# Adding into the residual by transfer: an attention projection, a branch and mixed streams in a two-layer kernel

## The chip, the cores and the metric

The kernel runs on one core of one Trainium2 chip. The metric is device time in microseconds (us) of one execution, and lower is better. The time before is the median of three runs.

## The reference

Two layers are applied to a residual `x` of shape 2 x 1024 x 512 (batch, token, channel), everything in 32-bit floats. In both layers an attention and a second part read the same layer-normalized `xn`, and both are added to `x`:

```python
xn = layernorm(x)
x = x + L0_attn(xn) + L0_ffn(xn)      # layer 0
xn = layernorm(x)
x = x + L1_attn(xn) + L1_ffn(xn)      # layer 1

def L0_attn(x):                       # one head of 128, no mask
    q, k, v = split(x @ Wqkv + bqkv)
    return softmax(q @ k.T / sqrt(128)) @ v @ Wo + bo

def L0_ffn(x):                        # 4 streams of 128 channels
    xr = x * rsqrt(mean(x * x) + eps)
    H_res  = sinkhorn(xr @ W_res.T + base, 50 iterations)   # 4 x 4 a token
    H_pre  = softmax(xr @ W_pre.T + ...)                    # 4 a token
    H_post = softmax(xr @ W_post.T + ...)                   # 4 a token
    H_res  = (1 - g) * I + g * H_res
    y      = sum_n H_pre[n] * x_stream[n] @ W_branch        # the branch
    return sum_j H_res[i, j] * x_stream[j] + H_post[i] * y  # streams i
```

Layer 1 is a causal attention with 32 query heads in 8 groups, whose keys and values come from a low-rank projection, over the 1024 tokens of each batch. Its second part is a linear layer with eight low-rank experts, of which each token takes two. These parts are not changed.

## The kernel before, in words

**Layout.** The residual lies in SBUF for the whole run as sixteen tiles `acc[b, t]` (batch b of 2, token tile t of 8), 128 tokens x 512 channels in 32-bit floats each, 256 KB. They are loaded with `x` and everything is added to them in place; the last addition to a tile is followed by its store. Matmuls are done on pairs of 16-bit floats (a high and a low part, three products for one), so that most results are written twice: once as the high part by ScalarE (ACT) and once as the low part by VectorE (DVE) or GpSimd (POOL).

**Order.** The program names the order; a scheduler that simulates the engines then fixes each engine's own order within the dependencies, so that an edit at one place can move instructions of every engine. Tiles come from pools with a fixed number of buffers by tag; a new tile of a tag waits until the oldest buffer's readers are done. The tag that matters here is `f2k` (128 x 512 in 32-bit floats, FB = 4 buffers). It serves, among others:

- the weights fetched by POOL's queue (`fetch`, L717) and split into high and low parts by POOL (`split_pool`, L97 to L99, behind a low part of a softmax row on DVE, L338)
- the attention output of layer 0 on its way to its two parts (`ao` in `attn0_out`, written at L502, read at L504 and L505)
- the normalized tile of batch 1 in layer 0 (`normed_T`, L242, then L247 on ACT and L249 on POOL or DVE, then a transposing transfer into `big`)
- the branch's products (`branch0_add`, L477) and the mixed streams (`stream_at`, L661).

**Layer 0, batch 0 and 1.** `front0` normalizes and projects to queries, keys, values and the logits of the 4 x 4 matrices. `attn0_rows` computes softmax rows: scores on PE (L91), exponentials on ACT (L300), the low parts on POOL (L336) or DVE (L338), transposes by transfer (into `PT`). `attn0_out`, once for each half of a batch, multiplies by the values (PE L373), and then for each of four token tiles multiplies with `Wo` (L510, L512) and adds the result from PSUM to the residual on DVE (L514). `branch0` computes `y` for each tile (ACT L463, POOL L464); `branch0_add` spreads it over the four streams on POOL (L477) and adds it on POOL (L481). For batch 0 the branch adds stand right behind the attention; for batch 1 they are spread over the first steps of layer 1, each behind a low part on DVE (`behind(..., True)` is a wait on that instruction).

The Sinkhorn iteration of batch 0 (`chain_dve`, L604 to L611; its kernels are recalculated once at L596) runs on DVE in small instructions between the other work of layer 0, and ends in `Hm[0]` (L555). That of batch 1 (`chain_pool`) runs on POOL and DVE in the first half of layer 1's first group.

**Mixing.** `mix0_units` loads a tile of `x` again, normalizes it, and adds the four streams, each weighted with its column of `Hm`. In one form ACT makes the four weighted copies of a stream (L661) and POOL adds them to the residual (L662); in the other, DVE does both in one instruction a copy (L670; ACT prepares a PSUM tile at L642). Batch 0 mixes at the end of layer 0: tiles 1, 3, 6 and 7 in the first form, the others in the second. Batch 1 mixes all eight tiles in the first form while layer 1 of batch 0 runs, and there every L662 waits behind a low part on DVE:

```python
add = G.tensor_tensor(acc[b, t], acc[b, t], m, ALU.add)      # L662
if b:
    behind(add, last_low[0], True)
```

**Layer 1** normalizes batch 0 (L242 again, then `big<-wo` transposes), and runs sixteen groups (two batches of eight) of 32 softmax steps; each step's place also carries the next group's weight fetches and splits, query projections, value products (`av`, L373), output blocks, and the extra work of the other batch. The padding of short softmax rows is written by POOL (`Phl`, L342) before the row is transposed (L343, issued by SyncE, SP).

Of the kernel before, what the change touches and what calls it, by code (L numbers as in the profile page):

```python
# [11 lines left out]
AF = mybir.ActivationFunctionType  # L12
ALU = mybir.AluOpType
# [3 lines left out]
P = 128  # L17
# [3 lines left out]
H = 512  # L21
# [7 lines left out]
FB, PB, LB, XB, WB = 4, 3, 3, 4, 9  # L29
# [25 lines left out]
def tile_model(ctx: ExitStack, tc: tile.TileContext, out: bass.AP, a: dict):  # L55
# [3 lines left out]
    V, A, G = nc.vector, nc.scalar, nc.gpsimd  # L59
# [7 lines left out]
    def T(tag, shape, dt=F32, bufs=None):  # L67
        count[0] += 1
        kw = {} if bufs is None else {"bufs": bufs}
        return sb.tile(shape, dt, tag=tag, name=f"{tag}_{count[0]}", **kw)  # L70
# [4 lines left out]
    def PP(shape=(P, 512)):  # L75
        count[0] += 1
        return ps.tile(list(shape), F32, tag="pp", name=f"pp_{count[0]}", bufs=BP)

    def bc(ap, axis, n):
        return ap.unsqueeze(axis).to_broadcast(  # L80
            [*ap.shape[:axis], n, *ap.shape[axis:]])
# [43 lines left out]
    acc = {}  # L125
# [60 lines left out]
    last_hi, last_lo, last_low = [None], [None], [None]  # L186

    def after(*insts):

        st = ExitStack()  # L190
        for i in insts:
            st.enter_context(tc.issue_after(i.ins))
        return st

    def behind(i, j, wait=False):

        kind = mybir.DependencyClass.Sync if wait else mybir.DependencyClass.NoSync
        tc.add_manual_dep(i.ins, j.ins.name, mybir.DependencyInfo(
            kind, mybir.DependencyReason.DATA), reason="behind")

    def rsqrt(y, ve, tag):

        t = T(tag, list(ve.shape), bufs=2)
        A.activation(t, ve, AF.Ln)
        A.activation(y, t, AF.Exp, scale=-0.5)
        V.tensor_tensor(t, y, y, ALU.mult)
        V.tensor_tensor(t, t, ve, ALU.mult)
        V.tensor_scalar(t, t, -0.5, 1.5, ALU.mult, ALU.add)
        V.tensor_tensor(y, y, t, ALU.mult)
# [51 lines left out]
    def srow():  # L261
        count[0] += 1
        return ps.tile([P, 512], F32, tag="s", name=f"s_{count[0]}", bufs=BS)
# [68 lines left out]
    def rows_lo(Pm, r, W, pool, hl, dst):  # L332
        whole, hi, los, pad = hl
        for a0, a1, lo in los:
            if pool:
                G.tensor_tensor(lo, Pm[:, a0:a1], hi[:, a0:a1], ALU.subtract)  # L336
            else:
                last_low[0] = V.scalar_tensor_tensor(lo, Pm[:, a0:a1], r[:, 1:2], hi[:, a0:a1],  # L338
                                                     ALU.mult, ALU.subtract)
        if pad is not None:  # L340

            behind(G.memset(pad, 0.0), last_low[0])  # L342
        nc.sync.dma_start_transpose(dst[:, :whole.shape[1] // P], whole)  # L343
# [17 lines left out]
    def out_tile():  # L361
        count[0] += 1
        return ps.tile([P, 512], F32, tag="av", name=f"av_{count[0]}", bufs=BV)

    def attn_out(p, Vh, PT, nj, mixed=None):


        full = nj - (mixed is not None)
        todo = [(Vh(j, l), PT(r * nj + j)) for j in range(full) for l, r in PASSES]
        if mixed is not None:  # L370
            todo += [(mixed(l), PT(full)) for l in range(2)]
        for k, (v, pt) in enumerate(todo):
            nc.tensor.matmul(p, v, pt, start=(k == 0), stop=(k == len(todo) - 1))  # L373
# [99 lines left out]
    def branch0_add(b, t, y4, hh):  # L473

        y = y4
        y4 = T("f2k", [P, 4, P], bufs=FB)
        mul = G.tensor_tensor(y4, bc(y, 1, 4), bc(hh[:, t, 1, :], 2, P), ALU.mult)  # L477
        if b:
            behind(mul, last_low[0], True)
        af = acc[b, t]  # L480
        G.tensor_tensor(af, af, y4.rearrange("p i c -> p (i c)"), ALU.add)  # L481

    def attn0_rows(b, half, Q, K, between=lambda: None):
        PTs = []
# [9 lines left out]
    def attn0_out(b, half, Vh, PTs):  # L494

        p = out_tile()
        for k in range(2):
            attn_out(p[:, 256 * k:256 * k + 256], lambda j, l: Vh[:, j, l, :],
                     lambda n: PTs[k][:, n].rearrange("p a b -> p (a b)"), NT)
        ao = T("f2k", [P, 512], bufs=FB)  # L500
        bv = bqkv[:, 2:3]
        A.activation(ao, p, AF.Identity, bias=bv, scale=1.0 / PSCALE)  # L502
        hl = T("wo", [P, 2, 512], F16, bufs=WB)
        A.activation(hl[:, 0], ao, AF.Copy)  # L504
        G.tensor_tensor(hl[:, 1], ao, hl[:, 0], ALU.subtract)  # L505
        for q in range(4):
            t = 4 * half + q
            p = PP()
            for r in range(2):
                nc.tensor.matmul(p, row, bo[:, r], start=(r == 0), stop=False)  # L510
            for k, (l, r) in enumerate(PASSES):
                nc.tensor.matmul(p, hl[:, l, q * P:(q + 1) * P], wo0[:, r, :],  # L512
                                 start=False, stop=(k == 2))
            V.scalar_tensor_tensor(acc[b, t], p, 1.0 / 1024.0, acc[b, t], ALU.mult, ALU.add)  # L514

    def sinkhorn(b, lg):

# [106 lines left out]
    def mix0_units(b, t, rs, pool):  # L624


        got = {}

        def load():
            if b == 0 and t >= 4:  # L630
                if t % 2 == 0:
                    xr_more[t] = T("P", [P, 2, H], bufs=PB)
                xr = got["xr"] = xr_more[t & ~1][:, t % 2]
            else:
                xr = got["xr"] = T("xr", [P, H], bufs=XB)
            with after(t0):
                nc.sync.dma_start(xr, a["x"][(b * NT + t) * P:(b * NT + t + 1) * P, :])
            if b == 0:
                A.activation(xr, xr, AF.Identity, scale=rs[:, 2, t:t + 1], bias=rs[:, 1, t:t + 1])
                if not pool:  # L640
                    got["d"] = srow() if t < 4 else PP()
                    A.activation(got["d"], acc[b, t], AF.Copy)  # L642
                return
            with tc.issue_after(p0.ins):
                behind(G.tensor_scalar(xr, xr, rs[:, 2, t:t + 1], rs[:, 1, t:t + 1], ALU.mult, ALU.add),
                       last_low[0], True)

        def stream(j):
            if b == 0 and (not pool or j > 1):
                with after(*(last_rs[:1] if pool else last_rs[1:] if j else last_mix)):  # L650
                    stream_at(j)
            else:
                stream_at(j)

        def stream_at(j):
            xj = got["xr"][:, j * P:(j + 1) * P]
            by = [Hm[b][:, t, i, j:j + 1] for i in range(NC)]
            if pool:
                m = T("f2k", [P, H], bufs=FB)
                for i in range(NC):  # L660
                    A.activation(m[:, i * P:(i + 1) * P], xj, AF.Copy, scale=by[i])  # L661
                add = G.tensor_tensor(acc[b, t], acc[b, t], m, ALU.add)  # L662
                if b:
                    behind(add, last_low[0], True)
                return

            for i in range(NC):
                sl = slice(i * P, (i + 1) * P)
                dst = acc[b, t] if j == NC - 1 else got["d"]
                last_stt[0] = V.scalar_tensor_tensor(dst[:, sl], xj, by[i], got["d"][:, sl], ALU.mult, ALU.add)  # L670

        return [load] + [lambda j=j: stream(j) for j in range(NC)]
# [384 lines left out]
    PTs = attn0_rows(0, 0, *f0[0][:2], lambda: adv(CA))  # L1057
    ys0 = branch0(0, *f0[0][3:5], lambda: adv(CB))
    attn0_out(0, 0, f0[0][2], PTs)
    PTs = attn0_rows(0, 1, *f0[0][:2], lambda: adv(CA))  # L1060
    attn0_out(0, 1, f0[0][2], PTs)
    for t in range(NT):
        branch0_add(0, t, ys0[t], f0[0][4])
# [3 lines left out]
    for half in range(2):  # L1067
        if half:
            kv0[1][0]()
            kv0[1][1]()  # L1070
        for hh in (2 * half, 2 * half + 1):
            load_q(0, hh)
        PTs = attn0_rows(1, half, *f0[1][:2], lambda: adv(CD))
        attn0_out(1, half, f0[1][2], PTs)
# [60 lines left out]
    for t in range(NT):  # L1135
        put(1, 2 * t, lambda t=t: branch0_add(1, t, y4s[t], f0[1][4]))
# [93 lines left out]
```

## Time and profile before

| | |
|---|---|
| median of three runs | 1851.93 us (1847.24, 1851.93, 1852.3) |
| the profiled execution, its time | 1847.82 us |
| its span | 1846.1 us, so 1.7 us lie around it |
| mean granted clock of PE | 0.976 |
| busy, PE | 1708.1 us (93%), 11394 matmuls |
| busy, DVE | 1473.8 us (80%) |
| busy, ACT | 1189.0 us (64%) |
| busy, POOL | 871.5 us (47%) |
| POOL L662 | 48 of median 1.272 us, 196.5 to 837.4 us |
| POOL L481 | 16 of median 1.277 us, 93.4 to 324.8 us |
| DVE L514 | 16 of median 0.681 us, 91.9 to 193.9 us |
| first PE matmul of layer 1 | at 223.38 us |

The profile is of one execution. Its page gives busy times, the span in 40 slices of 46 us with the busy tenths of each engine, DMA queues, the chain of work that ended last, and the costliest groups of instructions. The trace behind it answers for one stretch, line or wait. In a row of the timeline the first number is the start in us and the second the duration, "x3" counts instructions that follow each other, and the brackets give the idle time just before on that engine and the instruction that ended it. In a row of the waits the engine and instruction that waited stand first, then the releaser, then the total in us, the number of waits and the longest. POOL's issuing of DMAs (some 0.6 us each) is not counted as busy.

### The profile page before, as it was taken

The numbers are of one execution on the slowest core, as the hardware profiler recorded it, in microseconds if no ns is written. First come the engines' busy times: TensorE is split into PE (matmuls) and PEld (weight loads), VectorE is DVE, ScalarE is ACT, GpSimd is POOL, SyncE is SP. The second block draws the span as 40 slices with busy tenths as digits, with TensorE's granted clock in tenths as the row PEclk, the third lists the DMA queues.
The fourth block names the chain that finished last, engine by engine and source line by source line (L and its number), as shares of the span: only waits on it lengthen the run. The fifth ranks groups of instructions, "written<-read, shape, count | busy, mean of one in ns | idle before, by whom it ended". The sixth has DMA issues, their size and how long they took to land. (4 is left out here: it accounts for less than half of the span.)

```text
span 1846.1 us, 35011 instructions
## 1 busy us (share of the span) xinstructions
PE 1708.1 (93%) x11394; PEld 1038.2 (56%) x11394; DVE 1473.8 (80%) x4170; ACT 1189.0 (64%) x2917; POOL 871.5 (47%) x1460
## 2 busy tenths in 40 slices
PE   4666399999999999999999999999999999999998
PEld 2434146566666655566555566665666665665565
DVE  7988868888888877887577798898787877778675
ACT  3848656767665767886366667657566767666564
POOL 5568628878766464647254233324142323235200
PEclk9888699999999999999999999999999999999999
DMA  7435225756565656456484656557565665666455
GB/s 212 84 54 130 61 64 113 162 109 142 112 145 102 147 116 143 100 133 147 82 166 99 131 110 141 111 128 162 142 141 125 142 123 129 130 143 126 103 118 118
DMA packets 685034, 228.15 MB, mean 124 GB/s; under 512 B 665633, under 2 KB 665761, under 8 KB 684850
## 3 DMA queue, kind: packets, MB, share of 16 engines
q1 hardware_dynamic: 669394, 178.65, 47.2%
q0 software_dynamic: 13152, 43.07, 8.3%
q10 hardware_dynamic: 2304, 4.20, 0.7%
q8 instruction: 89, 1.46, 0.3%
q14 instruction: 95, 0.78, 0.2%
HBM read 52.81 MB, written 4.19 MB: 31 GB/s over the span
## 5 line engine op out<-in xcount | busy, mean ns | idle before, releaser
L300 ACT ACTIVATE P<-P,nm 128x1024 f32<-128x1024 f32 (+31 forms) x528 | 391.4, 742 | 278.1 <-DVE nm L292 253.4
L338 DVE SCALAR_TENSOR_TENSOR Phl<-P,r,Phl 128x64 f16<-128x64 f32 (+16 forms) x627 | 462.9, 763 | 79.0 <-ACT Phl L330 73.3
L91 PE MATMUL s<-K,Q 128*128 128x512 f16 (+22 forms) x2400 | 440.5, 317 | 19.8 <-DVE nm L292 10.5
L373 PE MATMUL av<-PT,V 128*128 128x256 f16 x3456 | 422.6, 273 | 12.2 <-DMA PT<-Phl 6.8
L373 PEld LDWEIGHTS <-V 128*128 128x128 f16 x3456 | 336.8, 98 | 95.1 <-DMA PT<-Phl 9.7
L330 ACT ACTIVATE Phl<-P,r 128x1024 f16<-128x1024 f32 (+31 forms) x515 | 368.8, 731 | 17.1 <-DMA PT<-Phl 2.0
L91 PE MATMUL pp<-wo,ao 128*128 128x512 f16 x1536 | 370.2, 380 | 3.3 <-ACT ao L107 3.2
L91 PE MATMUL pp<-big,wq 128*128 128x512 f16 x1536 | 368.6, 380 | 0.0
L97 POOL TENSOR_SCALAR f2k<-f2k 128x512 f32<-128x512 f32 x164 | 110.5, 675 | 512.3 <-DVE Phl L338 461.4
L91 PEld LDWEIGHTS <-Q 128*128 128x128 f16 x2400 | 223.9, 98 | 177.3 <-issue 29.6
L91 PEld LDWEIGHTS <-wq 128*128 128x128 f16 x1536 | 149.1, 98 | 166.8 <-issue 2.7
L91 PEld LDWEIGHTS <-ao 128*128 128x128 f16 x1536 | 149.7, 98 | 158.4 <-ACT ao L107 5.0
L91 PEld LDWEIGHTS <-big 128*128 128x128 f16 x1824 | 120.9, 99 | 87.8 <-DMA big<-wo 40.6
L292 DVE CUSTOM_DVE_ANT_0 P<-s,mask,nm 128x272 f32<-128x272 f32 (+15 forms) x256 | 157.7, 617 | 11.1 <-PE s L91 3.1
L296 DVE TENSOR_SCALAR_CACHE_REDUCE P<-s 128x512 f32<-128x512 f32 (+15 forms) x272 | 152.3, 562 | 11.9 <-PE s L91 10.4
L324 DVE RECIPROCAL r<-r 128x1 f32<-128x1 f32 x528 | 79.3, 155 | 78.6 <-ACT P L300 75.4
L325 ACT ACTIVATE r<-r 128x1 f32<-128x1 f32 x528 | 94.9, 192 | 68.3 <-DVE r L324 67.6
L107 ACT ACTIVATE ao<-av 128x512 f16<-128x512 f32 x128 | 75.0, 586 | 83.9 <-PE av L373 80.6
L342 POOL MEMSET Phl<- 128x192 f16 (+1 forms) x320 | 55.7, 189 | 153.0 <-DMA PT<-Phl 86.8
L292 DVE CUSTOM_DVE_ANT_0 P<-s,mask 128x32 f32<-128x32 f32 (+15 forms) x256 | 105.1, 430 | 19.0 <-PE s L91 18.6
L91 PE MATMUL pp<-big,big 128*128 128x128 f16 (+2 forms) x816 | 103.9, 283 | 17.5 <-DVE sk L606 12.7
L777 DVE SCALAR_TENSOR_TENSOR acc<-pp,acc 128x512 f32<-128x512 f32 x128 | 87.1, 681 | 31.6 <-PE pp L91 31.1
(266 smaller groups left out, 2064.3 us busy)
## 6 DMA issues: line engine op xcount, KB each, us to landing
f2k<-in_Wq POOLq DMA_DIRECT2D x64, 256.0 KB, 3.1
f2k<-in_WoT POOLq DMA_DIRECT2D x64, 256.0 KB, 3.3
PT<-Phl SPq DMA_TRANSPOSE x528, 3.2
acc<-in_x SPq DMA_DIRECT2D x16, 256.0 KB, 5.3
f2k<-in_Wup POOLq DMA_DIRECT2D x16, 256.0 KB, 3.4
xr<-V SPq DMA_DIRECT2D x32, 128.0 KB, 2.3
out<-acc ACTq DMA_DIRECT2D x16, 256.0 KB, 2.7
xr<-in_x SPq DMA_DIRECT2D x12, 256.0 KB, 5.1
```

The lines of the kernel that those rows point to most:

```text
L91: nc.tensor.matmul(dst, lhs(l), rhs(r), start=(i == 0 and j == 0), stop=(i == n - 1 and j == 2))
L97: first = G.tensor_scalar(stage, stage, scale, 1.0, ALU.mult, ALU.mult)
L107: A.activation(hl_hi, src, AF.Copy, scale=scale)
L292: last_row[0] = V.tensor_tensor_reduce(Pm[:, o:o + w], pt[:, :w], mask[:, 512 - w:], -scale, first, ALU.add, ALU.min, nm[:, k:k + 1])
L296: last_row[0] = V.tensor_scalar(Pm[:, o:o + w], pt[:, :w], -scale, first, ALU.mult, ALU.min, accum_out=nm[:, k:k + 1])
L300: A.activation(Pm[:, :W], Pm[:, :W], AF.Exp, bias=last, scale=-1.0, accum_out=r[:, 0:1])
L324: V.reciprocal(r[:, 1:2], r[:, 0:1])
L325: A.activation(r[:, 1:2], r[:, 1:2], AF.Copy, scale=PSCALE)
L330: A.activation(hl[1], Pm[:, :W], AF.Copy, scale=r[:, 1:2])
L338: last_low[0] = V.scalar_tensor_tensor(lo, Pm[:, a0:a1], r[:, 1:2], hi[:, a0:a1], ALU.mult, ALU.subtract)
L373: nc.tensor.matmul(p, v, pt, start=(k == 0), stop=(k == len(todo) - 1))
L777: V.scalar_tensor_tensor(acc[b, t], p, 1.0 / 256.0, acc[b, t], ALU.mult, ALU.add)
```

## The change

A helper issues a transfer on POOL's queue that adds its source to its destination. It is used at three places: for the projection of layer 0's attention (all sixteen tiles; ACT first copies the PSUM result, scaled, to an `f2k` tile), for the branch (all sixteen tiles) and for the mixed streams of batch 1 (32 transfers, four to each tile, without the wait behind DVE's low part). Batch 0's streams stay with POOL's addition. So 64 transfers of 256 KB from SBUF to SBUF are added, and 16 DVE instructions and 48 POOL additions go; 16 ACT copies come in. Two transfers to one tile follow each other by a wait on the first one's landing, and a source buffer is free when its transfer has landed.

```diff
+    def add_to(dst, src):
+
+        return G.dma_start(dst, src, accum_op=ALU.add)
+
...
     def branch0_add(b, t, y4, hh):
...
-        af = acc[b, t]
-        G.tensor_tensor(af, af, y4.rearrange("p i c -> p (i c)"), ALU.add)
+        add_to(acc[b, t], y4.rearrange("p i c -> p (i c)"))
...
     def attn0_out(b, half, Vh, PTs):
...
-            V.scalar_tensor_tensor(acc[b, t], p, 1.0 / 1024.0, acc[b, t], ALU.mult, ALU.add)
+            y = T("f2k", [P, H], bufs=FB)
+            A.activation(y, p, AF.Copy, scale=1.0 / 1024.0)
+            add_to(acc[b, t], y)
...
         def stream_at(j):
...
                 for i in range(NC):
                     A.activation(m[:, i * P:(i + 1) * P], xj, AF.Copy, scale=by[i])
-                add = G.tensor_tensor(acc[b, t], acc[b, t], m, ALU.add)
                 if b:
-                    behind(add, last_low[0], True)
+                    add_to(acc[b, t], m)
+                else:
+                    G.tensor_tensor(acc[b, t], acc[b, t], m, ALU.add)
                 return
```

## The prediction

> **What bounds the kernel now.** I read the 40 slices first, then the busy times by stretch, then the timeline of the stretch where PE isn't full, then the waits and the DMA rows.
>
> ```profile
> PE   4666399999999999999999999999999999999998
> DVE  7988868888888877887577798898787877778675
> ```
>
> The first five slices (some 230 us) are layer 0: PE is half idle and DVE, with the Sinkhorn chain of batch 0 between its other work, is the fullest engine. From slice six on PE is full. So a delay in layer 0 is paid in full, unless it disappears before PE's first matmul of layer 1, and a gain on DVE, ACT or POOL later is worth at most the little that PE idles there. The stretches give the sizes (columns: busy us of PE, PEld, DVE, ACT, POOL with counts, clock, DMA share, GB/s):
>
> ```profile
> 92.00:138.00 46.00, 28.34 (x197) 17.16 (x196) 40.04 (x137) 19.02 (x37) 28.85 (x27) 0.81 0.31 56
> 138.00:184.00 46.00, 32.04 (x236) 18.99 (x233) 40.53 (x134) 37.44 (x78) 37.12 (x43) 0.85 0.52 127
> 184.00:235.00 51.00, 20.63 (x97) 9.27 (x96) 46.07 (x141) 31.69 (x91) 32.72 (x34) 0.70 0.23 59
> 235.00:600.00 365.00, 355.80 (x2331) 215.59 (x2330) 294.56 (x831) 234.29 (x588) 254.39 (x532) 0.99 0.57 120
> 600.00:880.00 280.00, 269.22 (x1873) 167.07 (x1871) 221.84 (x583) 211.43 (x566) 158.25 (x232) 1.00 0.59 131
> ```
>
> The streams of batch 1 are mixed in 600 to 880: there PE idles 280 - 269.22 = 10.8 us. That is all that this part can win. In layer 0 the seam between the batches decides (timeline, POOL, then ACT, then PE; start, duration, instruction, idle before and releaser):
>
> ```profile
> 102.39 4.04 POOL L477 TENSOR_TENSOR f2k<-ao,hh 128x512 f32<-128x512 f32 x4
> 106.38 4.94 POOL L481 TENSOR_TENSOR acc<-acc,f2k 128x512 f32<-128x512 f32 x4
> 111.27 1.06 POOL L477 TENSOR_TENSOR f2k<-ao,hh 128x512 f32<-128x512 f32 x1
> 112.26 1.17 POOL L249 TENSOR_TENSOR wo<-f2k,wo 128x512 f16<-128x512 f32 x1
> ```
> ```profile
> 108.91 0.81 ACT L242 ACTIVATE f2k<-acc,rsa 128x512 f32<-128x512 f32 x1 [10.14 <-POOL acc L481]
> ```
> ```profile
> 116.68 1.58 PE L91 MATMUL pp<-big,big 128*128 128x152 f16 x11 [12.73 <-DVE sk L606]
> ```
>
> ACT's first normalized tile of batch 1 (L242) waits 10.14 us, because it wants one of the four f2k buffers and a branch add of batch 0 still reads it. After it come ACT L247, POOL L249, a transpose and PE's first matmul of batch 1, 7.8 us later. So f2k buffers, not arithmetic, set the start of batch 1, and the change makes every accumulated tile hold such a buffer until a DMA has landed.
>
> **Price of a landing.** No accumulating DMA and no SBUF-to-SBUF copy of 256 KB is in this trace. The nearest rows (KB each, median us from issue to landing):
>
> ```profile
> q0 software_dynamic: 13152, 43.07, 8.3%
> ...
> f2k<-in_Wq POOLq DMA_DIRECT2D x64, 256.0 KB, 3.1
> ...
> acc<-in_x SPq DMA_DIRECT2D x16, 256.0 KB, 5.3
> xr<-V SPq DMA_DIRECT2D x32, 128.0 KB, 2.3
> ```
>
> Low end 2.3 (a copy inside SBUF, half the bytes), high end 5.3 (sixteen loads in a burst). I take 4.0: POOL's own fetch of 256 KB at 3.1, and one more source read. Queue q0 used 8.3% of 1846.1 us for 43.07 MB, 164 pieces of 256 KB, so 153.2 / 164 = 0.93 us a piece, and 3.1 + 0.93 = 4.0. Issuing costs POOL some 0.57 us, as its fetches do (L717 in the timeline). The Trainium skill ("DMA: Bandwidth & Descriptors", "Anatomy of one DMA") gives a GpSimd-issued transfer as 2.0 us plus bytes over 436 GB/s, which I estimate at 2.6 us for 256 KB; the trace's 3.1 is above that, and by the page's figure the seam below would cost 6.3 us instead of 10.5 and the sum be 1852.6.
>
> **The seam, step by step.** I take the order from the changed program. PE's first product of the second half of batch 0 is ready at 101.87 (where L514 starts now). ACT copies it out (0.69, as the equal eviction L502 takes) to 102.56, and POOL issues the transfer; behind it in POOL's queue stand the branch products L477, which need that buffer back. It lands at 102.56 + 4.0 = 106.56. Three L477 of 1.03 run to 109.65, then the first branch transfer is issued; it lands at 113.65. The fourth L477 and three issues end at 112.96. The buffer freed at 113.65 takes the fifth L477 (to 114.68); the next two wait for 115.25 and follow each other to 117.31; the transfer of the fifth goes out then and lands at 121.31. Only there has L242 its buffer: 12.4 us later than 108.91. L242 and L247 (0.81 and 0.63) end at 122.75, L249 (no longer behind a late L477) at 123.9, and the transpose (3.3, as big<-wo takes) gives PE its tile at 127.2, against 116.68. **+10.5 us.** It is three landings in series, so 3 us for each us of landing: at 3.1 it is 7.8, at 5.3 it is 14.4, at 2.3 (where POOL's own work begins to bind) 5.9. Behind L242 on ACT's queue stands the recalculation of the Sinkhorn kernels (L596), so DVE stops there too, some 8 us.
>
> **What comes back before layer 1.**
>
> ```profile
> L514 DVE SCALAR_TENSOR_TENSOR acc<-pp,acc x16: 627/681/692, 91.9 to 193.9; 128x512 f32<-128x512 f32 x16
> ```
>
> These leave DVE, 16 x 0.68 = 10.9 us, and the program puts more Sinkhorn steps ahead of batch 1 (106 between the last row of batch 0 and its first L411, now 81 and eight L514), leaving three after the last L338 instead of about 28. Batch 1 takes as long from L411 to its last L338, so that L338 moves with the seam, from 177.34 to about 187.8, and Hm is ready near 191 instead of 195.6. But ACT begins to mix only behind the last eviction of batch 1's attention, which now is its own:
>
> ```profile
> 193.13 1.20 ACT L642 ACTIVATE pp<-acc 128x512 f32<-128x512 f32 x2 [3.29 <-DVE acc L514]
> ```
>
> That eviction follows the last L338 through transpose, PE L373 and L512, and so is late by the 10.5. Sixteen copies of 0.69 on ACT replace sixteen of 0.68 on DVE at the same place of that chain: no difference. What DVE mixes itself (L670, 195.64 to 204) may start up to 4 us sooner; I count -1.5, between -4 and 0, since PE's first matmul of layer 1 (223.38) waits for the tiles that ACT and POOL mix. Layer 0: +10.5 - 1.5 = **+9.0**.
>
> **Layer 1.** The eight branch adds of batch 1 become issues: POOL gets 0.7 us back for each, and it isn't the bound: nothing. For the mixing:
>
> ```profile
> POOL f2k L97 <- DVE Phl L338: 461.4, 82, 30.0
> ...
> POOL acc L662 <- DVE Phl L338: 55.9, 16, 9.5
> ```
>
> The second row is the wait that goes, the first how long weight splits wait on POOL anyway (5.6 us each). Now the 32 adds cost POOL 32 x 1.27 + 55.9 = 96.6 us. Afterwards the four transfers to one tile must follow each other: 32 issues x 0.57 + 24 landings x 4.0 = 114.2 at most, +17.6 us, less where ACT's next stream (four L661 of 0.39) or other POOL work fills the wait. Queued behind a waiting transfer are padding memsets (L342), which release the transposes for PE's L373, weight splits (L97 to L99) and fetches. POOL is busy 158 of 280 us there, and the splits have slack, so I count 0, between -10.8 (all PE idle time gone) and +17.6. The fetches of the whole kernel (L717) issue in 0.54 to 0.59 us, the longest in 0.76, beside a DVE that is 80% busy, so I take no more than 0.57 for an issue. The Trainium skill ("SBUF — State Buffer", "Who interferes with whom") speaks against the change here: a VectorE operation in a 2-port mode keeps GpSimd from writing the descriptors of its transfers; by that rule, with the longest issue of the trace as its sign, the 32 issues would cost POOL 32 x 0.17 = 5 us more, an estimate.
>
> **Sum.** The profiled execution took 1847.82, of which the span is 1846.1 and 1.7 lie around it. 1847.8 + 9.0 = 1856.8. The median of the three runs, 1851.93, is 4.1 above that execution, which by the same offset gives 1860.9; I name the middle, 1859. About 0.3% (5.5 us) can be told from no change: under 1846.4 is faster, over 1857.5 slower.
>
> **Rivals.** (1) *POOL's relief wins* (faster, 0.20): landings near 2.3, the DVE gain of 4 us in full, and PE's idle 10.8 us at the mix gone because the split and memset queues no longer stand behind L662's 55.9 us: 5.9 - 4 - 10.8 = -8.9, 1847.8 - 8.9 and half the offset of 4.1, about 1841. For it: POOL and DVE both lose work, and waits of up to 9.5 us go. Against: three landings in series are in the program's order, and PE's gaps at the mix are mostly released by DVE's nm and P. (2) *The seam is cheap and nothing else moves* (0.18): short landings, 5.9 - 4 = +1.9, likewise about 1852. For it: L242 already waits 10 us, and Hm comes earlier. (3) *POOL becomes the bound at the mix* (0.10): at 5.3 a landing, 32 x 0.57 + 24 x 5.3 = 145.4, 48.8 more than now; half of it seen by PE is +24, with 14.4 - 1.5 at the seam, about 1887. It decides from where a landing chain of four exceeds what POOL has free per tile, (280 - 158) / 8 = 15 us. Forecast (0.52): own range 1855 to 1872. The 0.52 with little of it under the bound, and 0.10, make slower 0.60; (2) and that little make same 0.20; (1) makes faster 0.20. Range: from the gains of (1) by half, 1846, to the seam at 14.4 with half of the 17.6, 1847.8 + 14.4 + 8.8 + 4.1 = 1875, so 1846 to 1876.
>
> **What the changed profile would show.** Right: accumulating transfers landing in 3 to 5 us; L242 of batch 1 starting near 121, with about 12 us more wait, released by a DMA; PE's first matmul of batch 1 near 127 and of layer 1 near 232; PE idle from there as much as now. Wrong: a landing under 2.3 or over 5.3; PE's layer 1 starting by 226; PE's idle time in the mix stretch different by over 5 us, with memsets or splits waiting behind transfers if it grows.

## The result, and the profile after

The changed kernel took 1906.84 us (median of four runs, 1901.7 to 1909.47) against 1850.77 of four runs before: ratio 1.0302, 95% interval 1.0275 to 1.0330, some 56 us slower. The profiled execution took 1901.7 us with a span of 1899.9. Lines after L197 have moved in the changed file: L338 is now L342, L242 is L246, L249 is L253, the branch's product L477 is L481 (which was its addition), L502 is L505, L661 is L666, L717 is L723; ACT's new copy of the projection is L518, and the accumulating transfer is L203.

The 40 slices of the changed kernel:

```profile
PE   4747379999999889989999999999999999999998
DVE  7978568888887747657666789899787878787776
```

Slices are 47.5 us now. PE's third slice has fallen from 6 to 4, its sixth from 9 to 7 (layer 1 starts later), and there are new dents at slices 14, 15 and 18, with DVE at 4 to 7 in slices 14 to 19, where it was at 7 and 8. Those are the mixing of batch 1. The stretches (the columns are those of before):

```profile
92.00:138.00 46.00, 17.59 (x132) 11.88 (x130) 33.00 (x111) 17.02 (x34) 32.35 (x33) 0.70 0.83 143
138.00:184.00 46.00, 36.93 (x263) 21.27 (x260) 41.53 (x149) 36.89 (x79) 29.60 (x33) 0.89 0.31 69
184.00:235.00 51.00, 18.08 (x82) 8.28 (x82) 26.81 (x85) 31.36 (x78) 36.10 (x36) 0.68 0.50 108
235.00:600.00 365.00, 349.71 (x2279) 210.07 (x2280) 299.00 (x845) 237.47 (x601) 257.54 (x541) 0.98 0.61 129
600.00:880.00 280.00, 249.48 (x1624) 150.01 (x1622) 179.81 (x496) 186.26 (x483) 109.73 (x185) 0.95 0.72 137
```

In 600 to 880 PE idles 30.5 us where it idled 10.8, at a granted clock of 0.95 instead of 1.00, while POOL is less busy than before (109.7 against 158.3). Nobody became the bound: the engines wait for each other. To place the loss in time I paired the records of the exponentials' line (ACT, L300 before, L304 after) by their number in both traces; an exponential leaves two records, and the first 32 are layer 0's. The 41st record is 19.2 us late, the 281st (at 623 us before) 13.7, the 401st 48.4, the 481st (at 954) 53.1, and from there it hardly changes to the end (53.9). So the loss has two places: **20 us before layer 1, of which 6 are made up by 620 us, and 39 in the mixing of batch 1.**

The 39 us are not idle time alone. Between the 281st and the 481st record PE runs nearly the same matmuls in both kernels (2216 before, 2220 after). Before, that takes 330.7 us, with PE busy for 319.9 and idle for 10.8 at a granted clock of 1.00; after, it takes 370.1 us, busy for 337.0 and idle for 33.1 at 0.95. So some 22 us are more idle time and 17 are the same matmuls taking longer, as the clock would have it (319.9 / 0.95 = 336.7). The lower clock comes with the idle time: over the same records the run with the streams alone, below, has 27.7 us idle at 0.96, and the one without the wait 3.8 us at 1.00. Which gaps lower it is not shown.

The seam between the batches (timeline of the changed kernel, POOL, ACT, PE):

```profile
100.87 3.53 POOL L203 DMA_DIRECT2D acc<-f2k  x4 [1.44 <-ACT f2k L518]
104.20 1.26 POOL L481 TENSOR_TENSOR f2k<-ao,hh 128x512 f32<-128x512 f32 x1
106.52 1.04 POOL L481 TENSOR_TENSOR f2k<-ao,hh 128x512 f32<-128x512 f32 x1 [1.06 <-DMA acc<-f2k]
...
108.84 0.86 POOL L203 DMA_DIRECT2D acc<-f2k  x1
...
112.09 4.48 POOL L481 TENSOR_TENSOR f2k<-ao,hh 128x512 f32<-128x512 f32 x3
116.52 0.85 POOL L203 DMA_DIRECT2D acc<-f2k  x1
```
```profile
119.85 0.81 ACT L246 ACTIVATE f2k<-acc,rsa 128x512 f32<-128x512 f32 x1 [5.71 <-DMA acc<-f2k]
```
```profile
126.18 1.07 PE L91 MATMUL pp<-big,big 128*128 128x152 f16 x7 [24.21 <-DMA big<-wo]
```

L246 stood at 108.91 and PE at 116.68: +10.9 and +9.5. Three rounds of landings follow each other on the way: those of the projection's transfers, issued from 100.87 on, release the first products (104.20 to 107.86); those of the first branch transfers, issued from 108.84 on, release the next three (112.09 on); that of the transfer at 116.52 frees L246's buffer at 119.85. The second place is at the end of layer 0 (POOL, ACT, PE):

```profile
197.24 0.57 POOL L723 DMA_DIRECT2D f2k<-in_Wup  x1 [2.64 <-DMA acc<-f2k]
199.61 0.55 POOL L723 DMA_DIRECT2D f2k<-in_Wq  x1 [1.79 <-DMA acc<-f2k]
201.49 0.89 POOL L203 DMA_DIRECT2D acc<-f2k  x1 [1.33 <-ACT f2k L518]
```
```profile
199.65 0.81 ACT L644 ACTIVATE P<-P,rsa 128x512 f32<-128x512 f32 x1 [1.61 <-DMA P<-in_x]
200.59 0.60 ACT L518 ACTIVATE f2k<-pp 128x512 f32<-128x512 f32 x1
205.26 0.69 ACT L505 ACTIVATE f2k<-av,bqkv 128x512 f32<-128x512 f32 x1 [4.07 <-DMA acc<-f2k]
```
```profile
243.44 3.76 PE L91 MATMUL s<-big,PT 128*128 128x512 f16 x10 [30.40 <-DMA big<-wo]
```

ACT's copy of the last attention output (L505, L502 before) wants the buffer of the fourth projected tile, whose transfer is issued at 201.49. On POOL two weight fetches that wait for landings themselves stand ahead of it, but what releases it is ACT's fourth copy (L518, 200.59), and that stands on ACT behind two tiles of reloaded `x` (L644) that waited 4.67 and 1.61 us for their load. L505 runs at 205.26 instead of 188.49, and PE's layer 1 starts at 243.44 instead of 223.38: +20.1.

In the mixing, the waits of 600 to 920 us (who waited for whom, total, times, longest):

```profile
DVE bnst L223 <- DMA acc<-f2k: 32.1, 8, 7.2
POOL acc L203 <- DMA acc<-f2k: 27.9, 8, 6.6
ACT f2k L666 <- DMA acc<-f2k: 21.7, 9, 5.8
```

All three engines that feed PE's softmax now wait for landings. One tile shows how it reaches PE (timeline: POOL, DVE, ACT, PE):

```profile
705.19 0.91 POOL L203 DMA_DIRECT2D acc<-f2k  x1
```
```profile
711.16 0.69 DVE L223 BATCH_NORM_STATS2 bnst<-acc 128x6 f32<-128x512 f32 x1 [7.17 <-DMA acc<-f2k]
```
```profile
714.30 0.75 ACT L304 ACTIVATE P<-P,nm 128x544 f32<-128x544 f32 x1 [9.89 <-DVE nm L296]
```
```profile
713.52 1.23 PE L91 MATMUL s<-K,Q 128*128 128x304 f16 x6 [3.54 <-DVE P L300]
```

The last of four transfers is issued at 705.19 and the statistics of the tile, which stand next on DVE, wait for its landing until 711.16. The maxima of the next rows stand behind them, ACT's exponentials behind those, and PE has no free score buffer.

What a transfer costs (DMA rows, then the issue line: duration min/median/max in ns):

```profile
acc<-f2k POOLq DMA_DIRECT2D x64, 256.0 KB, 4.3
```
```profile
L203 POOL DMA_DIRECT2D acc<-f2k x64: 848/895/1850, 91.7 to 880.2; - x64
```

### The profile page after: what moved, and what is told of

Its sections match the earlier page's. It is cut to its first block, busy times and chain, and to the rows that moved or that the text cites. A ratio compares the mean times of both kernels' runs of the same rounds, so it can differ in the third digit from the quotient of the medians.

```text
span 1899.9 us, 35088 instructions
## 1 busy us (share of the span) xinstructions
PE 1723.8 (91%) x11394; PEld 1043.4 (55%) x11394; DVE 1452.6 (76%) x4154; ACT 1198.8 (63%) x2933; POOL 854.8 (45%) x1476
## 3 DMA queue, kind: packets, MB, share of 16 engines
q0 software_dynamic: 22368, 59.85, 14.0%
## 5 line engine op out<-in xcount | busy, mean ns | idle before, releaser
L304 ACT ACTIVATE P<-P,nm 128x1024 f32<-128x1024 f32 (+31 forms) x528 | 391.3, 741 | 288.7 <-DVE nm L296 274.8
L342 DVE SCALAR_TENSOR_TENSOR Phl<-P,r,Phl 128x64 f16<-128x64 f32 (+16 forms) x627 | 445.0, 735 | 80.1 <-ACT Phl L334 71.2
L91 PE MATMUL s<-K,Q 128*128 128x512 f16 (+22 forms) x2400 | 445.1, 319 | 31.4 <-DVE P L300 15.6
L377 PE MATMUL av<-PT,V 128*128 128x256 f16 x3456 | 428.4, 276 | 13.7 <-DMA PT<-Phl 13.2
L334 ACT ACTIVATE Phl<-P,r 128x1024 f16<-128x1024 f32 (+31 forms) x515 | 369.6, 731 | 20.1 <-DMA PT<-Phl 5.1
L296 DVE CUSTOM_DVE_ANT_0 P<-s,mask,nm 128x272 f32<-128x272 f32 (+15 forms) x256 | 157.4, 616 | 10.9 <-PE s L91 3.2
L300 DVE TENSOR_SCALAR_CACHE_REDUCE P<-s 128x512 f32<-128x512 f32 (+15 forms) x272 | 152.5, 563 | 11.7 <-PE s L91 10.3
L346 POOL MEMSET Phl<- 128x192 f16 (+1 forms) x320 | 63.1, 225 | 160.9 <-DMA PT<-Phl 99.7
L91 PE MATMUL pp<-big,big 128*128 128x128 f16 (+2 forms) x816 | 104.3, 285 | 28.6 <-DMA big<-wo 27.2
```

The source lines that it names most:

```text
L91: nc.tensor.matmul(dst, lhs(l), rhs(r), start=(i == 0 and j == 0), stop=(i == n - 1 and j == 2))
L296: last_row[0] = V.tensor_tensor_reduce(Pm[:, o:o + w], pt[:, :w], mask[:, 512 - w:], -scale, first, ALU.add, ALU.min, nm[:, k:k + 1])
L300: last_row[0] = V.tensor_scalar(Pm[:, o:o + w], pt[:, :w], -scale, first, ALU.mult, ALU.min, accum_out=nm[:, k:k + 1])
L304: A.activation(Pm[:, :W], Pm[:, :W], AF.Exp, bias=last, scale=-1.0, accum_out=r[:, 0:1])
L334: A.activation(hl[1], Pm[:, :W], AF.Copy, scale=r[:, 1:2])
```

## The experiments

Each is compared with the kernel before, run on the same chip. "Lag" is again the lateness of the 281st and the 481st of these records against the trace of before, which frames the mixing; it comes from one profiled execution each. The one of before took 1847.82 us where the median is 1850.77, so a lag of a few us is no reading by itself.

**Each part alone.** The three parts of the diff, one at a time; nothing else is changed.

> Only the projection of layer 0's attention goes by accumulating transfer; branch and streams are added by POOL as before. Theory H (buffers held until landing, at two seams of layer 0, and DVE's statistics waiting for landings at the mix): the second seam (second half of batch 1: ACT's copy of the attention output waits for the landing of a transfer that stands behind two fetches on POOL) is all here, about +10 at PE's first matmul of layer 1, and a part of the first seam (one of its three landings in series), +2 to +4. So layer 1 starts 10 to 14 us later than at 223.4, the time is +6 to +12 (some of the lag is made up before 620 us), and nothing is lost between 620 and 900. Rival Q (transfers on POOL's queue hold up POOL's other work wherever they are): the start of layer 1 moves by less than 6. Rival R (any edit that moves the schedule costs this much): the loss lies in 620 to 900 as well, over 15 us.

Measured 1867.38 us, ratio 1.0097 (1.0081 to 1.0113), +17. PE's layer 1 starts at 242.87, 19.5 late, nearly as in the whole change, and the lag doesn't grow in the mixing (19.2, 20.0). Rivals Q and R are out, but Theory H's sizes missed too (+6 to +12, and layer 1 late by 10 to 14), and the seam was wrongly shared out: PE's first matmul of batch 1 comes at 127.89, so the projection alone makes 11.2 of it. Its trace shows why. Before, three branch products (L477) had their f2k buffers at 90.4, ahead of the second half's projection; now the projection's eight tiles take the buffers and all eight products follow at 104, where POOL works them and their additions off one after the other, and L246 (118.86) waits for such an addition and not for a landing.

> Only the branch goes by accumulating transfer. Theory H: two landings in series at the first seam instead of two POOL additions of 1.3 us on the same buffer, +3 to +7 at PE's first matmul of batch 1 (116.7 before) and as much at the start of layer 1; the eight transfers of batch 1 cost nothing; the time is +2 to +7. Rival Q: the eight transfers in layer 1 hold up weight splits behind them, so another +5 or more between 235 and 340 us. Rival R: over 15 us lost in 620 to 900.

Measured 1855.64, ratio 1.0028 (1.0014 to 1.0042), +5, a time as Theory H had it, but otherwise spread: PE's first matmul of batch 1 is only 2.0 late (118.73), the last normalized tiles wait longer, and layer 1 starts at 231.88, 8.5 late. With a lag of 5.5, then 7.1, neither rival is seen.

> Only the mixed streams of batch 1 go by accumulating transfer, without the wait behind DVE. Theory H: layer 0 as before (layer 1 starts at 223 to 224), and the loss of the whole change in 620 to 900 us is here: +30 to +42. DVE waits some 30 us, eight times, for a landing before the statistics of a tile. Rival R (the parts do harm only together, through f2k buffers that all of them share): less than +15. Rival C (it is the lag of layer 0 that pushes the mix against other work): also less than +15.

Measured 1883.17, ratio 1.0192 (1.0169 to 1.0215), +33. Lag 1.1, then 33.6. DVE waits 28.6 us in eight times for landings. Theory H held, and both rivals are out. The three parts add up to 17 + 5 + 33 = 55 of the 56, which is chance in part: in layer 0 they don't add (layer 1 starts 19.5 late for the projection and 8.5 for the branch, but 20.1 for both, and the lag at the 281st record is 19.2, 5.5 and 1.1 alone against 13.7 together), and the mixing loses 32.5 for the streams alone and 39 in the whole change.

**Statistics after the mix.** The streams alone, with

```diff
     def late_stats(t):
...
-        norm_stats(1, ln1[1][0], t)
+        with after(last_low[0]):
+            norm_stats(1, ln1[1][0], t)
```

> As the run with the streams alone, but the statistics of batch 1's tiles are issued on DVE behind the last low part at their place in the program, after the mix, and not early. Theory H: DVE no longer waits for landings (under 5 us instead of some 30), and 15 to 35 us of the loss of the streams alone come back: +0 to +20 against before. Rival Q (splits, memsets and ACT's buffers behind the landings on POOL's queue make the loss): it stays within 6 us of the streams alone. Rival C (transfers slow the others): the same, and transposes land later than 3.2 us.

Measured 1876.33, ratio 1.0143 (1.0122 to 1.0164), +26. DVE's wait at the statistics is gone, and 7 us came back of the 15 to 35 expected. Of its waits of 600 to 900 us those for landings on POOL and ACT have grown:

```profile
POOL acc L203 <- DMA acc<-f2k: 35.0, 9, 7.7
...
ACT f2k L665 <- DMA acc<-f2k: 22.6, 10, 5.1
```

So the plainest wait of the profile was not the cause by itself. That ACT and POOL stood still at the same time anyway would explain it; the runs without the chain and with a fifth buffer, below, bear on that.

**No transfers, no wait.** The kernel before, with only the wait taken away:

```diff
-                add = G.tensor_tensor(acc[b, t], acc[b, t], m, ALU.add)
-                if b:
-                    behind(add, last_low[0], True)
+                G.tensor_tensor(acc[b, t], acc[b, t], m, ALU.add)
```

> No transfer adds anything: POOL adds the streams of batch 1 itself as before, but no longer behind the low part on DVE, so that the scheduler places streams and statistics nearly as in the run with the streams alone. Theory H (the landing, and what waits for it in program order on DVE and ACT, makes the loss of the streams): within 8 us of before, on either side. Rival R (the new order alone, with statistics and streams earlier and not spaced by DVE's rows, makes it): +15 to +33 against before.

Measured 1843.51, ratio 0.9947 (0.9930 to 0.9963): 9 us faster than before, just outside what was expected. Streams and statistics stand in the order that they have with the transfers, the four streams of a tile in a row and its statistics behind, so that Rival R is out (lag 3.2, then -5.0), and what the wait had cost is won. In PE's terms the stretch 620 to 880 of this run is

```profile
620.00:880.00 260.00, 256.18 (x1816) 160.63 (x1815) 204.00 (x563) 203.41 (x550) 154.43 (x229) 1.00 0.62 138
```

with 3.8 us of PE idle time; it was 249.22 busy before and is 229.48 in the changed kernel. Against this run the streams' transfers cost 33 + 9 = 42 us.

**Copies instead of additions.** The whole change with

```diff
-        return G.dma_start(dst, src, accum_op=ALU.add)
+        return G.dma_start(dst, src)
```

> The whole change, but the 64 transfers copy onto the residual's tiles and do not add to them (the sums are left out). Order, waits and buffers stay. Theory H: what costs is that a transfer lands some 4 us after its issue, whatever it does; without the second read it lands near 3.3 instead of 4.3, and a fifth to a third of the 56 us goes: +36 to +48 against before. Rival A (the adding itself is what is dear, in the DMA engines' time and in the issue of 0.9 us): landings near 2.5, issue near 0.6, and more than half of the loss goes: under +28.

Measured 1871.03, ratio 1.0097 (1.0062 to 1.0133), +18. Two thirds of the loss go with the adding, as Rival A had said. Its DMA row and issue line:

```profile
acc<-f2k POOLq DMA_DIRECT2D x64, 256.0 KB, 2.7
```
```profile
L203 POOL DMA_DIRECT2D acc<-f2k x64: 538/562/592, 92.3 to 853.4; - x64
```

A copy of the same 256 KB lands in 2.7 us and not 4.3, and its issue takes 0.56 and not 0.90. The first seam shrinks from 9.5 to 5.4 (122.06), the start of layer 1 from 20.1 to 12.2 (235.55), the mixing from 39 to 17 (lag 8.4, then 25.6). The loss falls faster than the landing, by 67% against 37%. Landing, issue and the transfers' share of the DMA engines all fall together here, so which of them makes the adding dear is not shown.

**Other buffers for the second seam.** The projection alone, with

```diff
-            y = T("f2k", [P, H], bufs=FB)
+            y = T("ao", [P, H], bufs=2) if b else T("f2k", [P, H], bufs=FB)
```

> As the run with the projection alone (+16.9), but batch 1's eight copies of the projection go to the two buffers of another tag (ao), so that ACT's copy of the attention output and the weight fetches find f2k buffers free. Theory H: PE's first matmul of layer 1 comes 7 to 11 us earlier than in that run, and the time is +5 to +10 against before; the copies now wait for each other's landing, which costs 2 to 4 us. Rival Q (POOL's queue, not the buffer, is late there): within 3 us of +16.9.

Measured 1857.62, ratio 1.0028 (1.0013 to 1.0044), +5 as Theory H had it, and layer 1 starts 4.8 us earlier than in the projection's own run, where 7 to 11 were expected:

```profile
238.06 2.29 PE L91 MATMUL s<-big,PT 128*128 128x512 f16 x5 [22.47 <-DMA big<-wo]
```

The transfers are the same; only the buffers are others, and 12 of the 17 us are gone. Of these the start of layer 1 explains 4.8; the rest shows right behind it, where the 41st record is 9.8 late against 18.9. PE's first matmul of batch 1, which is batch 0's part, stays late (128.27).

**The chain broken.** The streams alone with late statistics, each stream added to another tile, so that no transfer follows one to the same tile:

```diff
-                    add_to(acc[b, t], m)
+                    add_to(acc[b, (t + 2 * j) % NT], m)
```

> As the run with the streams alone and late statistics (+25.8), but stream j of tile t is added to tile t + 2j (mod 8), so that no transfer waits for the one just before it (the sums go to other tiles). Theory H: POOL's waits for landings (35 us) and ACT's for buffers (22.6 us) fall to under 10 us each, and the loss to +0 to +10. If it stays within 5 us of +25.8, neither the chain of landings nor the buffers held by it make the loss, and what is left is the transfers' issue on POOL, their DMA time or the order.

Measured 1863.64, ratio 1.0063 (1.0040 to 1.0085), +12, against +26 with the chain. POOL no longer waits for landings before a transfer, but before its fetches (26.5 us in seven times), and ACT waits nearly as before (19.4 us in eight). The expectation was half right: breaking the chain gives 14 us back, and the rest stays while buffers are held.

**A fifth buffer**, for three runs, FB from 4 to 5 and XB from 4 to 3:

> As the run in which POOL adds the streams itself without the wait (1843.5, ratio 0.995), but with five f2k buffers instead of four, paid for by one of the four xr buffers. It is the measure for the next two. Both theories: within 6 us of that run, since there no buffer is held for long.

Measured 1868.40, ratio 1.0094 (1.0070 to 1.0118): the trade of an xr buffer for an f2k buffer costs 27 us against the run without the wait, outside the mixing (lag 10.4 at the 281st, 7.6 at the 481st, 21.8 at the 561st record). The expectation failed. As a measure for the next two only the mixing itself can be used, and there this run gains 2.8.

> As the run with the streams alone and late statistics (+25.8), with five f2k buffers and three xr buffers. Theory H (buffers held until landing stop ACT and POOL's fetches): ACT's waits for landings fall from 22.6 to under 10 us, and 5 to 12 us come back: +14 to +21. Theory D (the transfers' own work: q0 takes 29 to 30% of the DMA engines in this stretch instead of 11%, transposes land 0.4 us and fetches 1 us later, and an issue holds POOL 0.9 us): within 4 us of +25.8.

Measured 1901.06, ratio 1.0274 (1.0255 to 1.0293). Lag 11.8, then 42.7: +30.9 in the mixing. ACT's waits fell to 7.3 us, as Theory H said, and nothing came back: POOL's wait in the chain grew to 45.8 us in twelve times. With the chain in place a fifth buffer doesn't help: against POOL's additions with the same buffers the transfers cost 33 us here, and 35 with four buffers (+26 and -9). The sizes of both theories were given without the cost of the trade and can't be held to the time itself.

> As the unchained run (+11.6; the sums go to other tiles), with five f2k buffers and three xr buffers. Theory H: what was left there was POOL's fetches (26.5 us) and ACT (19.4 us) waiting for buffers, so it falls to +0 to +5. Theory D: it stays at +8 to +14.

Measured 1871.20, ratio 1.0108 (1.0090 to 1.0127), 3 us over the run with five buffers and POOL's additions. Lag 8.5, then 7.1: the mixing loses nothing, with the same 32 transfers, a transpose landing at 4.3 us instead of 3.2, and q0 at 30.5% of the DMA engines in 620 to 880 as in the chained run (30.9%). Theory D is out for this form. ACT's wait for buffers fell from 19.4 to 3.5 us, POOL's before its fetches only from 26.5 to 22.8: it is ACT's wait that goes with the loss, and Theory H was right in that half alone.

> POOL adds the streams itself without the wait (1843.5), and beside that 32 accumulating transfers of 256 KB, four for each tile, add the reloaded x to rows of the output in HBM that the final stores overwrite; nothing in the mixing waits for them. Theory D: POOL loses 32 issues of 0.9 us and the DMA engines the same share, so +10 to +20 against the run without them. Theory H: transfers that nobody waits for cost little, 0 to +6.

Measured 1865.11, ratio 1.0076 (1.0058 to 1.0093), 24 us over the run without the wait, more than either theory gave. The lag goes from 1.8 to 21.7. Here POOL has its own 32 additions and 32 issues in bursts of four, the transfers end in HBM and land in 6.8 us, and PE waits for transposes (PE L373 for PT<-Phl, 16.6 us in nine times, against 1.2 in two). The transfers are not quite without a waiter either, since they read the xr buffers: one reload of `x` waits 3.2 us for such a landing. Whether the late padding on POOL, the burst or the held xr buffers make the loss isn't settled; it shows that a load that no addition waits for isn't free either where POOL also adds.

**Batch 1's projection only**, through the ao buffers; batch 0's stays on DVE:

```diff
-            V.scalar_tensor_tensor(acc[b, t], p, 1.0 / 1024.0, acc[b, t], ALU.mult, ALU.add)
+            if b:
+                y = T("ao", [P, H], bufs=2)
+                A.activation(y, p, AF.Copy, scale=1.0 / 1024.0)
+                add_to(acc[b, t], y)
+            else:
+                V.scalar_tensor_tensor(acc[b, t], p, 1.0 / 1024.0, acc[b, t], ALU.mult, ALU.add)
```

> Only batch 1's projection goes by accumulating transfer, its eight copies through the two ao buffers; batch 0's stays on DVE. Theory H (what costs is f2k buffers that a landing keeps): PE's first matmul of batch 1 is back at 116 to 118 us, that of layer 1 within 3 us of 223.4, and the time within 4 us of before, on either side; the +5 of the run in which both batches go by transfer was batch 0's. Rival Q (transfers on POOL's queue cost wherever they are): PE's layer 1 starts 5 us late or more.

Measured 1847.07, ratio 0.9987 (0.9975 to 0.9998), no difference of weight. PE's batch 1 is back at 116.36, and

```profile
224.69 2.72 PE L91 MATMUL s<-big,PT 128*128 128x512 f16 x6 [25.50 <-DMA big<-wo]
```

Eight accumulating transfers into the residual, landing in 3.7 us, cost nothing that can be measured where no scarce buffer and no consumer waits for them.

**Fewer waits, no transfers.** The run without the wait at the streams, then also without `behind` at the branch's products, then also without that at the normalization of the reloaded x (L645):

> No transfers. POOL adds streams and branch as before, without the waits behind DVE's low parts at the streams' additions and at the branch's products. The first alone gave 1843.5 (ratio 0.995). If the waits cost by holding POOL's queue, this is as good or 1 to 3 us better: 1840 to 1844. If they protect DVE's rows from POOL's reads, it is 1 to 6 us worse: 1844 to 1850.

> As the run before, and also without the wait at the normalization of the reloaded x (L645, which waited 18.7 us in six times in the profile of before). By the same two readings: 1838 to 1844, or 1844 to 1852.

Measured 1841.13, ratio 0.9951 (0.9936 to 0.9965), and 1844.48, ratio 0.9966 (0.9954 to 0.9978). Both beat the two kernels. The first is where the reading of a held queue put it, the second between the two readings, and neither can be told from taking away the wait at the streams alone (0.9947). The gain is in that one wait; POOL's additions did not need to go.

## Why the prediction was wrong, step by step

**The price of a landing** (4.0, between 2.3 and 5.3) held in the median, 4.3 (3.8 in the mixing), but not as a bound: the 64 landed in 3.2 to 7.4, and 15 of them later than 5.3. The working, a fetch plus one more read of 0.93, held too: by q0's share, (14.0% of 1899.9 - 8.3% of 1846.1) / 64 = 1.76 us of the 16 engines a transfer, against 1.86. **The issue** was mis-sized: 0.57 was taken from fetches, 0.90 was measured. The plain copy at 0.56 shows that it is the adding. The Trainium skill's figure ("DMA: Bandwidth & Descriptors", "Anatomy of one DMA"), which gave an estimate of 2.6 us, fits the copy (2.7) and not the accumulating transfer; the measurement decides for the latter. Of the lock-out of GpSimd by VectorE that the prediction priced there is no sign: the longest issue is 0.592 for the copy, and 0.922 at a median of 0.875 for the 32 streams alone. The 1.85 in the whole change is the end of a burst, whose records overlap (three take 2.96 us from 110.41 on).

**The seam**, +10.5 by the sum and +9.5 measured, was right in size and in its path. L246 ran at 119.85, predicted 121.31, and the trace shows the three rounds of landings in series; in the run with plain copies they are shorter, and L246 comes at 116.19. But the parts show that landings are not the only way to this delay: the projection alone gives 11.2, with one landing and POOL's eight products and eight additions behind it, and the branch alone 2.0. The projection's run and the whole change share that the projection's tiles take the buffers, so that three of the eight products lose the place that they had at 90.4 and POOL makes all eight after 104.

**"What comes back before layer 1"** failed: -1.5 was predicted, +10.6 measured (20.1 - 9.5). The sentence that sixteen copies on ACT replace sixteen DVE instructions "at the same place of that chain: no difference" looked at their time and not at their buffers. The copies take f2k buffers until landing, and ACT's next attention output wants the fourth. The fourth transfer stands behind fetches on POOL that want such buffers back, which decides in the projection's own run (the copy ends at 198.55, the fetches go out at 198.65 and 199.93, the transfer at 200.47); in the whole change its copy comes last, behind ACT's wait for the reloaded `x`. The two-buffer run, where layer 1 starts 4.8 us earlier, and the run with batch 1's projection alone, where it starts at 224.69, show that the buffers matter; the two-buffer run still starts 14.7 us late, with batch 0's seam in it (11.6). Of the 20 us, 6 were made up later, which the prediction had not expected either ("a delay in layer 0 is paid in full"); the projection alone makes up none (18.9, then 19.2).

**Layer 1** failed most, and is the step that makes the prediction wrong: 0 was counted, between -10.8 and +17.6, and the mixing lost 39. The step added up POOL's time (96.6 before, 114.2 after) and found slack there, and POOL indeed had it: it was less busy than before. The loss sits with those who wait for a landing in their own program order, DVE at the statistics, ACT for its next buffer, POOL for its next transfer and next fetch. None of these waits is in the trace of before, so they could not be read from a row, but each could have been listed by asking of the landing: who reads this tile next, and who wants this buffer next. The step also had no term for PE's clock: 17 of the 39 us are the same matmuls at 0.95 instead of 1.00. Rival 3, whose price was 48.8 us more on POOL, half of it on PE, came nearest in size (+24 there, 39 measured), by another mechanism: POOL's free 15 us a tile did not matter.

What decides in the mixing, by the profiled executions (loss between the 281st and the 481st record): four buffers and chained +26.3, four unchained +19.7, five chained +30.9, five unchained -1.4; with POOL's additions -8.1 for four and -2.8 for five. Either the chain or the scarce buffers alone cost most of it, and only without both is it gone. The times say the same: the three forms that lose are 35, 20 and 33 us behind POOL's additions with as many buffers, the fourth 3. The orders differ a little from run to run, so that these are sizes and not shares. The unchained forms add to other tiles, which also moves the moment at which a tile is whole.

**Rival 1's half-truth.** That the wait of POOL behind DVE (55.9 us) costs PE something was right: taking it away gives 9 us, near the 10.8 of the rival. The change lost it again to landings.

## What to carry to other kernels

An accumulating transfer doesn't take work away, it turns 1.3 us on an engine into 0.9 us of issue and 4.3 us during which its source buffer, its destination and the next transfer to that destination are held; before making such a change, list for each transfer who wants the buffer next, who reads the destination next, and what stands behind those on their engines. It is free where a buffer is idle and the reader is far away (batch 1's projection through the ao buffers), and dear where four go to one tile out of a pool of four that weights also use. Before replacing an instruction that waits, take the wait away alone: here that was the whole gain, 0.5%. And price a stall of PE above its length: here 22 us of idle time came with 17 us of slower matmuls.

## What the runs showed that I had not expected

An accumulating transfer of 256 KB between SBUF tiles takes 0.895 us to issue on POOL against 0.562 for a copy, makes 144 packets against 80 (q0: 22368 and 18272 against 13152, over 64), and takes 1.76 us of the 16 DMA engines against 0.79. One f2k buffer more was not worth one xr buffer less: that trade alone cost 27 us.
